# A first layer whose matrix work is woven more finely into its turning steps, with pinned statistics and joined additions

## The chip, the cores and the metric

One Trainium2 chip, one of its cores. The metric is the device time of one execution in microseconds (us). A core has five engines with instruction queues of their own: TensorE (PE in the profile; its weight loads are PEld), VectorE (DVE), ScalarE (ACT), GpSimd (POOL), and SyncE (SP), which here issues DMAs. [...] SBUF is the working memory on the chip, PSUM the memory into which TensorE writes, in 8 banks of 512 floats for each of 128 partitions.

## The reference, cut to what matters

The network has four layers, each `x = x + layer(group_norm(x))`, on x of 8 images of 56 x 56 positions and 192 channels, in float32. The change is in the first layer alone. Cut to it:

```python
x = gn(x)                                   # 32 groups of 6 channels, per image
p = silu(x @ p_w.T + p_b)                   # 576 channels each
q = silu(x @ q_w.T + q_b)
v = silu(x @ v_w.T + v_b)
qv = q * v
o1 = toeplitz(qv along w, a1)               # per channel a causal-anticausal filter of the row
o2 = toeplitz(qv along h, a2)               # and of the column; a1, a2 from a small MLP
x = x_in + (p * (o1 + o2)) @ o_w.T + o_b
```

The filters are per channel 56 x 56 Toeplitz matrices, so `o1 + o2` is, for each channel and image, two small matrix products.

## The kernel before

**Tiles and stages.** The layer goes image by image (`b`, 8 of them), and in an image through the 576 channels of qv in nine slices of 64, taken two at a time: five steps `c` = 0 to 4, of which c = 4 (the *tail*) has one slice. A step of the loop has these parts:

- `turn_both` (L404; for the tail `turn`, L423, transposes L433, copies L440): seven steps of 8 rows of the product qv. Each has 16 TensorE transposes (L414) into one PSUM tile, and two copies out of it, by VectorE into `ol` and by ScalarE into `or` (L419). The two copies of one tile follow each other.
- `project` (L342): the *gates* of the next step's q and v. For each of four groups `g` of 392 x 2 positions, two PSUM tiles (q and v; one, holding both in its halves, for the tail) of six matmuls each (L358, twelve rows in the profile, as each float32 matmul is shown twice), then Silu by ScalarE (L369) into `s` tiles, then the products `multiply` (L378): one in `straight` order by VectorE (L381), two `across` by POOL (L387); of the last group POOL does one half of the latter and VectorE the other (L387 as well).
- `convolve` (L444): the Toeplitz products, 64 small matmuls in a PSUM tile (L457), two tiles for each slice; tile 0 is evicted into `ot` by VectorE (L477), tile 1 by ScalarE (L475); both engines (L468) for the tail. Each reads everything that was turned.
- `post` (L488), made after c = 1 and c = 3, each time for the four slices of two steps: gate p (L499, L506), turn back and multiply (`back`, L518, L523), output projection (`out`, L532; `rest`, L553; `alone`, L564), and additions into the accumulators `acca` and `accb` (`add`, L481). It runs beside the turning of the next step (c = 2 and c = 4). `post_tail` (L596) does the same for the tail, beside the turning of the next image's c = 0: `gates` (L606, matmuls L612, Silu L618), `back` (L627, L632), `out` (L640), `rest` (L655), with twelve additions (L486), each for one parity of image rows.
- `normalize` (L668) of the next image's x runs in c = 2, in three parts: `measure` (12 `bn_stats`, L156), `deviate` (aggregates L160, mean L161, spreading matmuls L129, variance), `last` (matmuls L129, Sqrt L170, reciprocal L171, L172, then the affines L49 and L680). `tell` (L686) measures the finished image for the next layer: 11 `bn_stats` in c = 0, its `deviate` and `last` in c = 1.

**PSUM.** Tiles are pairs of banks: three buffers `c`, taken in turn, and one `o`. `banks()` (L204) gives an `o` for each fourth tile while `ring["wide"]` holds (c = 0, 1, 3), and only `c` in c = 2 and 4, where `out` has the `o`. The gates' results and the gated p lie in six `s` buffers of SBUF.

**What sets the order.** TensorE's order in this layer is the program's (L712): it is written out with `merge` (L699), which spreads two lists of steps over each other. Within a pass of the loop: `merge(fill + early gates, turns)`, where `fill` are the steps of `post` or `post_tail`; then the early groups' products; then the other groups of `project`, merged with `beside` (parts of `tell` and `normalize`); then the convolutions, each second one followed by the DMAs that fetch the next Toeplitz tables (`toeplitz`, L324, L334). Before, two groups of gates were *early*, and only where there was no `fill` (c = 1 and c = 3, and the very first c = 0). At c = 3 the remaining groups alternate with convolutions. The order of VectorE, ScalarE, POOL and SP is chosen when the program is built, by a scheduler that reorders what the dependencies allow; each queue is then fixed and runs in order. Semaphore waits are inserted by the framework.

**Lines that move.** In SP's queue of an image's c = 0 are the store of the finished accumulators (L71), the load of the next image (L89), the load of the new accumulators (L73), and the Toeplitz tables for later convolutions (L334).

The core of the loop, as it was:

```python
early = [] if fill else ahead[0:2]
ring["wide"] = c not in (2, 4)
merge(fill + [f for f, _ in early], turns)
ring.update(at=0, wide=True)
for _, f in early:
    f()
ahead = whole(ahead[len(early) :])
```

Of the kernel before, what the change touches and what calls it, by code (L numbers as in the profile page):

```python
# [99 lines left out]
class GroupNormSplit:  # L100
# [40 lines left out]
    def steps(self, *spans):  # L141
# [12 lines left out]
        def measure(x, n, st, j):  # L154
            w = x.shape[-1] // n
            nc.vector.bn_stats(st[:, j, :], x[:, j * w : (j + 1) * w])  # L156
# [21 lines left out]
def layer0(cx, xin, xout, w, consts):  # L178
# [15 lines left out]
    with ExitStack() as es:  # L194
# [147 lines left out]
        def project(xn, q):  # L342
# [9 lines left out]
            def gates(g):  # L352
                pss = []
                for i in range(len(js)):
                    ps = banks()
                    for k in range(3):
                        for h, rows in enumerate(halves):
                            nc.tensor.matmul(  # L358
                                ps[:, h, 0:n], wqv[q][rows, k, i, :],
                                xn[rows, k, g * n : (g + 1) * n],  # L360
                                start=(k == 0), stop=(k == 2),
                            )
                    pss.append(ps)
                ts = []
                for i in range(2):
                    j, ps = js[0 if tail else i], pss[0 if tail else i]
                    rows = slice(i * DS, (i + 1) * DS) if tail else slice(0, 128)
                    t = work(2, n)[0 : DS if tail else 128]
                    nc.scalar.activation(t, ps[rows, :, 0:n], AF.Silu, bias=bqv[rows, j : j + 1])  # L369
                    ts.append(t)  # L370
                state[g] = ts
# [4 lines left out]
            return [(lambda g=g: gates(g), lambda g=g: products(g)) for g in range(4)]  # L376
# [219 lines left out]
        def post_tail(xn, ot, acc):  # L596
# [6 lines left out]

            sps, pos = [], []

            def gates():  # L606
                for g in range(2):
                    ps = banks()
                    for k in range(3):
                        for p in range(2):  # L610
                            for h in range(2):
                                nc.tensor.matmul(  # L612
                                    ps[sides[p], h, 0:n], wps[2][sides[h], k, 0, 0:DS],
                                    rows(xn[sides[h], k], g * 7, p),
                                    start=(k == 0), stop=(k == 2), skip_group_check=True,
                                )
                    sp = work(2, n)
                    nc.scalar.activation(sp, ps[:, :, 0:n], AF.Silu, bias=bp[:, NC - 1 : NC])  # L618
                    sps.append(sp)
# [15 lines left out]
            def out(g):  # L635
                po = pos[g]
                for h in range(2):
# [6 lines left out]
                    for p in range(2):  # L644
                        add(
                            0, NC - 1, rows(acc[0], h * 14 + g * 7, p),
                            pa[:, p, 0:n].rearrange("p (i w) -> p i w", w=H),
                        )

            def rest(g):  # L650
# [8 lines left out]
                for p in range(2):  # L659
                    add(  # L660
                        1, NC - 1, rows(acc[1], g * 7, p),
                        pb[:, p, 0:n].rearrange("p (i w) -> p i w", w=H),
                    )

            steps = [lambda f=f, g=g: f(g) for f in (back, out) for g in range(2)]
            return [gates, *steps, lambda: (rest(0), rest(1))]

        def normalize(xn):  # L668
# [7 lines left out]
            def last():  # L676
                rstd, nbias = settle(banks)
                for k in (0, 2):
# [7 lines left out]
        def tell(b, xa, xb):  # L686
# [3 lines left out]
            def last(bank):  # L690
                nn = cx.tile(gn.small, [128, 2, 2], "nn")
                for i, v in enumerate(settle(bank)):
                    nc.vector.tensor_copy(nn[:, :, i], v)
# [23 lines left out]
        def whole(steps):  # L717
            return [lambda f=f, h=h: (f(), h()) for f, h in steps]
# [1501 lines left out]
```

## Time and profile before

| | |
|---|---|
| median of 3 runs | 4062.32 us (4058.22 to 4072.35) |
| the profiled execution | 4069.0 us, its span 4067.2 |
| mean granted TensorE clock | 0.981 |
| TensorE busy in the span | 3786.1 us (93%) |
| weight loads | 2655.7 us (65%) |
| VectorE | 2371.5 us (58%) |
| ScalarE | 1789.6 us (44%) |
| POOL | 1523.3 us (37%) |
| images of the first layer, from one c = 0's first turning step to the next | 235.0, 234.9, 235.3 us (images 2 to 4) |
| the same for TensorE busy | 219.7, 218.1, 219.3 us |
| one `bn_stats` of 392 elements (L156) | 0.545 us; four in a row 1.96 |
| one gate's Silu (L369), 784 elements | 0.91 us |
| a turned tile's copies (L419) | VectorE 1.21, ScalarE 1.01 us |
| an activation table load | 1.283 us |
| VectorE's straight product (L381) | 0.97 us, 1.6 beside POOL |
| POOL's across product (L387), 392 elements | 1.93 us mean |
| the tail's additions before (L486, 392 elements) | 0.55 us, in a row 0.49 |

The times are of one profiled execution, from the span's start. In the groups and the timeline a row names line, engine, operation, output and inputs, and the idle time of the engine just before with what ended it. The matmuls' ends are modelled, so a TensorE row may overlap the next by 0.1 to 0.2 us. The first layer fills the span to about 1940 us.

### The profile page before, as it was taken

To read this page: it belongs to the slowest core of one execution; us is meant where nothing else is said; L and a number is where in the kernel's file an instruction comes from. 1 tells how busy PE (TensorE), PEld (TensorE's weight loads), DVE (VectorE), ACT (ScalarE), POOL (GpSimd) and SP (SyncE) were. 2 spreads that over 40 slices of the span, in tenths; PEclk is the share of its full clock that TensorE was granted. 3 is DMA by queue.
4 is the path that set the end of the run, shared out by engine and by line. 5 is a ranking of instruction groups with operands and counts; after the bars stand their busy time and mean duration, and the time that the engine had idled before them with its cause. 6 is when DMAs were issued, how large, how long until landed. Compare 5 with 4: busy or idle time off the path is not lost. (4 is left out here: it accounts for less than half of the span.)

```text
span 4067.2 us, 115859 instructions
## 1 busy us (share of the span) xinstructions
PE 3786.1 (93%) x51036; PEld 2655.7 (65%) x51036; DVE 2371.5 (58%) x3318; ACT 1789.6 (44%) x2021; POOL 1523.3 (37%) x1325
## 2 busy tenths in 40 slices
PE   6989999999998999999799999899989999998997
PEld 4777767677776767777566666444435455556997
DVE  6556565655657565555544444565566667665654
ACT  2434444344444434443334433243335555554564
POOL 3222242222233222223433333333334444444776
PEclk9999999999999999999899999999999999999999
DMA  7865353533526352342333443556557766653333
GB/s 158 169 143 131 81 142 103 125 77 98 125 76 160 85 136 72 89 105 76 108 104 103 107 104 94 167 166 209 166 163 184 181 153 154 153 132 102 99 99 98
DMA packets 390300, 507.94 MB, mean 125 GB/s; under 512 B 176932, under 2 KB 326724, under 8 KB 388404
## 3 DMA queue, kind: packets, MB, share of 16 engines
q1 hardware_dynamic: 385621, 494.07, 47.6%
q8 instruction: 401, 6.57, 0.7%
q10 hardware_dynamic: 3135, 3.47, 0.3%
q0 software_dynamic: 1040, 2.99, 0.3%
q14 instruction: 103, 0.84, 0.1%
HBM read 344.69 MB, written 155.65 MB: 123 GB/s over the span
## 5 line engine op out<-in xcount | busy, mean ns | idle before, releaser
L387 POOL TENSOR_TENSOR qv<-s,s 128x392 f32<-128x392 f32 (+3 forms) x320 | 569.3, 1806 | 1296.4 <-ACT s L369 1048.5
L358 PE MATMUL c<-x,wqv 64*128 64x392 f32 x2856 | 518.3, 509 | 45.9 <-ACT or L419 24.7
L358 PEld LDWEIGHTS c<-x,wqv 64*128 64x128 f32 x2856 | 285.0, 193 | 223.6 <-ACT or L419 29.8
L369 ACT ACTIVATE s<-c,bqv 128x784 f32<-128x784 f32 (+1 forms) x270 | 244.9, 913 | 330.0 <-PE c L358 308.1
L381 DVE TENSOR_TENSOR qv<-s,s 128x784 f32<-128x784 f32 (+1 forms) x160 | 229.0, 1441 | 132.0 <-ACT s L369 132.0
L499 PE MATMUL c<-x,wp 64*128 64x224 f32 x2688 | 282.1, 356 | 17.0 <-ACT s L506 14.4
L419 DVE COPY ol<-c 56x1024 f32<-56x1024 f32 x184 | 218.7, 1208 | 113.6 <-PE c L414 113.6
L499 PEld LDWEIGHTS c<-x,wp 64*128 64x128 f32 x2688 | 254.5, 189 | 21.7 <-ACT s L506 16.6
L523 DVE TENSOR_TENSOR s<-s,c 128x896 f32<-128x896 f32 x112 | 121.8, 1088 | 239.6 <-ACT s L506 233.3
L419 ACT COPY or<-c 56x1024 f32<-56x1024 f32 x184 | 184.0, 1008 | 175.8 <-DVE ol L419 169.5
L457 PEld LDWEIGHTS c<-or,ol 120*64 120x64 f32 x7168 | 217.3, 139 | 40.4 <-issue 38.0
L457 PE MATMUL c<-or,ol 120*64 120x56 f32 x7168 | 225.3, 224 | 19.3 <-issue 10.1
L2084 POOL TENSOR_TENSOR y<-y,s 128x448 f32<-128x448 f32 x168 | 185.2, 1102 | 95.8 <-ACT s L2063 95.8
L1552 ACT ACTIVATE vb<-sm 128x1024 f32<-128x1024 f32 (+1 forms) x100 | 103.9, 1040 | 261.1 <-issue 218.2
L2053 PE MATMUL h<-ringv,am 128*64 128x57 f32 (+1 forms) x4400 | 192.7, 235 | 21.8 <-DVE ringv L2040 13.9
L506 ACT ACTIVATE s<-c,bp 128x448 f32<-128x448 f32 x224 | 129.7, 630 | 185.5 <-PE c L499 184.1
L1541 PE MATMUL v<-wvb,wa 128*128 128x512 f32 (+1 forms) x400 | 192.1, 613 | 6.4 <-ACT wa L1427 6.4
L2053 PE MATMUL h<-ringh,am 128*64 128x57 f32 (+1 forms) x4400 | 186.3, 232 | 8.8 <-DVE ringh L2059 8.8
L2053 PEld LDWEIGHTS h<-ringv,am 128*64 128x64 f32 x4400 | 168.1, 140 | 25.4 <-DVE ringv L2040 14.9
L1060 PE MATMUL c<-wv,xc 128*126 128x192 f32 x896 | 175.4, 339 | 0.0
L2053 PEld LDWEIGHTS h<-ringh,am 128*64 128x64 f32 x4400 | 166.3, 139 | 11.1 <-DVE ringh L2059 11.1
L1570 POOL TENSOR_TENSOR l<-vb,ta 128x512 f32<-128x512 f32 (+1 forms) x52 | 75.2, 1446 | 259.5 <-ACT vb L1552 258.5
(268 smaller groups left out, 7708.7 us busy)
## 6 DMA issues: line engine op xcount, KB each, us to landing
or<-tt SPq DMA_DIRECT2D x252, 196.0 KB
ol<-tt SPq DMA_DIRECT2D x252, 196.0 KB
vt<-v SPq DMA_DIRECT2D x56, 672.0 KB
v<-vb SPq DMA_DIRECT2D x96, 384.0 KB
x<-x SPq DMA_DIRECT2D x110, 168.0 KB
wqv<-in_l_w_qv SPq DMA_DIRECT2D x38, 384.0 KB
x<-in_x SPq DMA_DIRECT2D x64, 196.0 KB
x<-x SPq DMA_DIRECT2D x110, 112.0 KB
```

The source lines that it names most:

```text
L358: nc.tensor.matmul(ps[:, h, 0:n], wqv[q][rows, k, i, :], xn[rows, k, g * n : (g + 1) * n], start=(k == 0), stop=(k == 2),)
L369: nc.scalar.activation(t, ps[rows, :, 0:n], AF.Silu, bias=bqv[rows, j : j + 1])
L381: nc.vector.tensor_tensor(sub(qv[rows, 7 * g :, 64 + H - 1 :], (HH * 120, 2), (120, 7), (-1, H)), *(t.rearrange("p u (h w) -> p u h w", w= ...
L387: eng.tensor_tensor(sub(qv[rows, w0:, H - 1 - 7 * g - HH * u :], (120, w1 - w0), (-1, 7)), *(t[:, u].rearrange("p (h w) -> p w h", w=H)[:, ...
L419: copy(dst[:, :, :, i0 : i0 + 8], view[rows])
L457: nc.tensor.matmul(ps[u * 64 : (u + 1) * 64, k, v * H : (v + 1) * H], left[:, d * H : d * H + 64], right[:, d * H : (d + 1) * H], start=Tr ...
L499: nc.tensor.matmul(ps[:, h, u * n : (u + 1) * n], wps[j][rows, k, u, :], xn[rows, k, g * n : (g + 1) * n], start=(u == 0 and k == 0), stop ...
L506: nc.scalar.activation(sp[:, u].rearrange("p (h i) -> p h i", h=2), ps[:, :, u * n : (u + 1) * n], AF.Silu, bias=bp[:, 2 * j + u : 2 * j + ...
L1060: nc.tensor.matmul(out(i, u), group(i, u), wv[0], start=(u == 0), stop=True, skip_group_check=True,)
L1541: nc.tensor.matmul(out, x[:, at : at + n], wt, start=(k == 0), stop=(k == 1), skip_group_check=True,)
L2053: nc.tensor.matmul(ps[sides[c], y], am[a][:, m * CB : (m + 1) * CB], old[:, x], start=(n < 2), stop=True, skip_group_check=True,)
L2084: nc.gpsimd.tensor_tensor(v, v, line[:, j], ALU.add)
```

## The change

- **Gates tile by tile.** `project` returns for each group a list of gate steps, one for each PSUM tile, where one step did both tiles. In the tail's gates the one tile is followed by its two Silus as before.
- **More early groups, and in another place.** The number of early groups now depends on c alone: two for c = 0 and 1, three for c = 3, none for 2 and 4. So c = 0 of every image has two early groups beside the tail's `post_tail`. The early gates are first merged with `fill`, then the result with the turning steps.
- **The tail's stage.** `post_tail`'s two gate tiles become two steps. `out` and `rest` add both parities of rows in one instruction of 784 elements, so twelve additions become six.
- **Statistics pinned.** Each `bn_stats` of `gn.steps` is pinned behind everything that the program has traced for VectorE before it. So those of the next image stand in c = 2, behind group 0's product, where the scheduler had placed them in c = 0; those of the finished image stand behind the products of groups 2 and 3 in c = 0.
- **ready.** After the reciprocal of the statistics, ScalarE applies Silu to one element of it, pinned in ScalarE's order. This puts the Silu table's load behind the Sqrt at once; before, it came with the next Silu that was needed. It is done in `normalize` and, except for the last image, in `tell`.

The number of TensorE, POOL and SP instructions is the same; VectorE has 48 fewer, ScalarE 15 more. The queues of VectorE, ScalarE and SP come out in another order: among others, in c = 1 both early straight products stand ahead of the copies of the last two turned tiles, and in c = 0 one stands ahead of the copy of turning step 4 and one ahead of that of step 6; in SP's queue of c = 0 the new accumulators' load stands behind the Toeplitz tables, where it stood ahead of them.

```diff
         def measure(x, n, st, j):
             w = x.shape[-1] // n
-            nc.vector.bn_stats(st[:, j, :], x[:, j * w : (j + 1) * w])
+            cx.tc.keep_in_program_order(
+                nc.vector.bn_stats(st[:, j, :], x[:, j * w : (j + 1) * w])
+            )
...
-            def gates(g):
-                pss = []
-                for i in range(len(js)):
-                    ps = banks()
-                    for k in range(3):
...
-                    pss.append(ps)
-                ts = []
-                for i in range(2):
...
-                    ts.append(t)
-                state[g] = ts
+            def gate(g, i):
+                ps = banks()
+                for k in range(3):
...
+                j = js[i]
+                for rows in halves if tail else [slice(0, 128)]:
                     t = work(2, n)[0 : DS if tail else 128]
                     nc.scalar.activation(t, ps[rows, :, 0:n], AF.Silu, bias=bqv[rows, j : j + 1])
+                    state.setdefault(g, []).append(t)
...
-            return [(lambda g=g: gates(g), lambda g=g: products(g)) for g in range(4)]
+            return [
+                ([lambda g=g, i=i: gate(g, i) for i in range(len(js))], lambda g=g: products(g))
+                for g in range(4)
+            ]
...
+            def pairs(x, r0):
+                return x.rearrange("q (i p w) -> q p i w", p=2, w=H)[:, :, r0 : r0 + 7, :]
...
-                    for p in range(2):
-                        add(
-                            0, NC - 1, rows(acc[0], h * 14 + g * 7, p),
-                            pa[:, p, 0:n].rearrange("p (i w) -> p i w", w=H),
-                        )
+                    add(
+                        0, NC - 1, pairs(acc[0], h * 14 + g * 7),
+                        pa[:, :, 0:n].rearrange("q p (i w) -> q p i w", w=H),
+                    )
...
-            steps = [lambda f=f, g=g: f(g) for f in (back, out) for g in range(2)]
-            return [gates, *steps, lambda: (rest(0), rest(1))]
+            steps = [lambda f=f, g=g: f(g) for f in (gate, back, out) for g in range(2)]
+            return [*steps, lambda: (rest(0), rest(1))]
+
+        def ready(v):
+            t = cx.tile(gn.small, [1, 1], "ready")
+            tc.keep_in_program_order(nc.scalar.activation(t, v[0:1, 0:1], AF.Silu))
...
                 rstd, nbias = settle(banks)
+                ready(rstd)
...
-                early = [] if fill else ahead[0:2]
+                early = ahead[0 : {0: 2, 1: 2, 3: 3}.get(c, 0)]
                 ring["wide"] = c not in (2, 4)
-                merge(fill + [f for f, _ in early], turns)
+                woven = []
+                merge(
+                    [lambda f=f: woven.append(f) for f in fill],
+                    [lambda f=f: woven.append(f) for fs, _ in early for f in fs],
+                )
+                merge(woven, turns)
```

## The prediction

> **What bounds the kernel now.** I read the page's busy shares, then one image of the first layer in windows, then the timelines of TensorE, VectorE and ScalarE around each place where TensorE idles, then the granted clock.
>
> ```profile
> PE 3786.1 (93%) x51036; PEld 2655.7 (65%) x51036; DVE 2371.5 (58%) x3318; ACT 1789.6 (44%) x2021; POOL 1523.3 (37%) x1325
> ```
>
> ```profile
> 1000.20:1235.10 234.90, 218.13 (x3160) 171.86 (x3156) 142.88 (x174) 102.07 (x120) 70.94 (x40) 0.99 0.42 107
> ```
>
> The second view is one image of the first layer (c=0's first turning step to the next image's): length, then busy us and instructions of PE, PEld, DVE, ACT, POOL, the granted clock, the DMA share, GB/s. TensorE works 218 of 234.9 us, VectorE 143, ScalarE 102, POOL 71. So TensorE's queue sets the time, and a change counts only where it opens or closes a TensorE gap. The layer runs to about 1940 us; the other three follow it and are only shifted. Per image the gaps sit in five places, the same in every image to 0.1 us: c=0's turning stage and the wait behind it (3.74 + 0.74), c=1 behind the turning (1.86), c=2's start (2.2) and end (0.52 + 0.84), c=3's turning (0.61 + 1.17 + 1.25), c=4 (0.3); and a gap of 2.0 to 3.25 in c=0's convolutions in images 1 to 6.
>
> ```profile
> 919.87 0.69 PE L414 MATMUL c<-ident,qv 64*120 64x64 f32 x16 [1.17 <-ACT s L369]
> ...
> 921.82 3.88 PE L358 MATMUL c<-x,wqv 64*128 64x392 f32 x12 [1.25 <-ACT or L419]
> ...
> 1039.49 1.20 PE L457 MATMUL c<-or,ol 120*64 120x56 f32 x33 [3.25 <-issue]
> ...
> 1056.65 4.22 PE L358 MATMUL c<-x,wqv 64*128 64x392 f32 x24 [1.86 <-ACT or L419]
> ...
> 1076.95 1.28 ACT L506 ACT_TABLE_LOAD   x1 [1.61 <-PE c L499]
> ...
> 1079.45 2.54 PE L499 MATMUL c<-x,wp 64*128 64x224 f32 x24 [1.65 <-ACT s L506]
> ...
> 1145.61 2.25 PE L358 MATMUL c<-x,wqv 64*128 64x392 f32 x12 [0.84 <-DVE ot L477]
> ```
>
> The columns are start, length, engine, line, operation, operands, count, and the idle time before with what ended it. The reader sees, in c=3 (the first two rows), turning steps that wait for ScalarE, and twelve gate matmuls that take 3.88 us where a later dozen takes 2.25; in c=1 a gate waits for a PSUM buffer until VectorE (1.22 us) and then ScalarE (1.01 us) have copied a turned tile; in c=2 the activation table load delays the first gate's Silu, and so the next gate by 1.65.
>
> The place that decides is c=2, where the next image is normalized:
>
> ```profile
> 1025.11 1.96 DVE L156 BATCH_NORM_STATS2 st<-x 128x6 f32<-128x392 f32 x4
> ...
> 1029.30 2.14 PE L358 MATMUL o<-x,wqv 64*128 64x392 f32 x12
> ...
> 1123.05 0.98 DVE L381 TENSOR_TENSOR qv<-s,s 128x784 f32<-128x784 f32 x1 [3.80 <-ACT s L369]
> ...
> 1123.81 2.14 PE L358 MATMUL o<-x,wqv 64*128 64x392 f32 x12
> ...
> 1125.78 1.62 PE L129 MATMUL c<-mean,gmat 64*128 64x1 f32 x28
> ...
> 1127.45 0.16 DVE L137 COPY spread<-c 128x3 f32<-128x3 f32 x1 [3.42 <-PE c L129]
> ```
>
> The mean's matmuls (L129) start without a gap, because their input was ready 93 us earlier: the statistics of x (L156) ran at 1022 to 1033, in c=0, beside full TensorE work.
>
> **What the Trainium skill says.** "TensorE: Matmul & The Clock Gate", "Part 1: The HAM clock gate", has TensorE at half rate after an idle window of about 3.4 us. The trace agrees on the length (records of 3.413 us at half clock, one from 921.7 to 925.1, under the 3.88 us row) and is finer: in this layer half of a window idle is enough. Windows 0.47 to 0.71 idle were followed by a half one; each costs about 3.4/2 = 1.7 us. The same page ("Architectural detail") has VectorE and ScalarE as strict queues and only weight loads pulled ahead on TensorE; the trace shows no exception. "SBUF — State Buffer", "Who interferes with whom": a VectorE instruction with two SBUF inputs contends with a POOL instruction that reads SBUF. The trace agrees: L381 takes 0.97 alone and 1.6 beside POOL's L387. "ScalarE: Activation LUTs", "What ACT_TABLE_LOAD costs": about 1283 ns plus a drain; the trace has 1283 and no drain (1076.95 to 1078.24).
>
> **The change part by part**, in the instruction order of the built program. n counts images.
>
> *Statistics pinned.* The 12 L156 of the next image now stand in c=2, behind the product L381 of gate group 0, followed by 3 aggregates and the mean; TensorE's order there is unchanged (groups 0 and 1, then the mean's matmuls). VectorE can't pass L381, which ends at 1124.0. Four L156 take 1.96, so 12 take 5.85: 1129.85. Aggregates 3 x 0.22, mean 0.16 (POOL is through by 1130.3): 1130.8. TensorE is there at 1125.95, so it stands for 4.85 us, with every later matmul behind it. n = 7 (images 0 to 6): **+34**. If the mean copy takes 0.73, as once in c=0, it is +37; at the least, with aggregates overlapped, +31. The clock: a 4.85 us gap always leaves one window over half idle, in most positions two; averaged over its position a half window behind it costs 1.7: **+12** (7 to 17). Taking 5.85 us of L156 from c=0 gives nothing, since TensorE waits for no VectorE work there.
>
> *The tiny Silu (ready).* It moves the Silu table load up behind the Sqrt. In c=2's start the 1.28 us load goes. Image 0, which has no statistics to finish there, shows what is late next: its stage idles 1.41, not 2.20. So -0.8, n = 7: **-5.5**; two half-clock windows there (behind 840 and 1550 us) go: **-3.4**. In c=2's end the load lies under the wait of 2.45 us for nbias; group 3's products come 1.28 earlier, the eviction L477 ends before TensorE asks, 0.84 goes, n = 7: **-6**. Its cost: ScalarE waits for the reciprocal (1072.1), so L475 starts 1.4 us late; its buffer isn't asked for before 1086. At the program's start, two L156 leave the chain to the first affine: **-1**.
>
> *Gates among turning steps, c=1.* TensorE's order becomes gate, turn, gate, turn, turn, gate, turn, turn, gate, turn, turn. But VectorE's order has both early products L381 ahead of the last two turned tiles' copies, and the second waits for the fourth gate's activation. Walking the queues with 1.97 a gate, 0.51 a turn, 1.2 + 1.0 a tile's two copies, times from the stage's first gate: the fourth gate ends at 10.65, its Silu (behind a turn's copy) at 12.4; L381 beside POOL to 14.05; the copy of turn 5 to 15.2, ScalarE's to 16.2. The next group's first tile waits 0.9 for its buffer, its second 1.8. The same walk with the order of before gives 1.6 where 1.86 is seen. So 2.7 for 1.86, n = 8: **+7** (-8 if the product found no wait).
>
> *c=0, the tail's stage.* Four gates (7.9 us of TensorE) move between the turns. VectorE's work there is about as long as before (six additions of 0.95 for twelve of 0.49; two L156 out, two L381 in), so a stage bound by VectorE becomes one bound by TensorE, up to its end. The walk finds two waits: 1.4 at the second image half of `out`, behind product 0 and turn 4's copies, and 3.0 for group 2's first gate, as product 1 waits for the last gate and turn 6's copies (1.2 + 1.0) queue behind it. Against 4.48 before, less what a later start takes: group 2 starts 1.2 earlier. n = 7: **-8.5** (-25 to 0). A gap of 3.0 makes a half window in some 8 of 10 positions, where two of 7 had one: **+6**. The additions alone save at most six starts, nothing on TensorE's path.
>
> *c=3.* A third early gate needs two ScalarE activations (1.83) among copies of 1.0: ScalarE binds. The walk has the convolutions end at 22.65 behind the stage's start against 22.9: n = 8, **-2**. Half windows there in 5 of 8 images become rarer and partly hidden: **-5**. POOL's products start with the last turning step as before, in every stage, and take 15.7 us (14.5 here); the next turning asks for them 20 us later in c=0 and c=1, but only some 15 later here: the cover is 1 to 2 us.
>
> *SP's queue.* The loads of the next accumulator (12 DMAs, 2.4 MB) fall behind the 16 table loads, and so out of the stretch in which c=0's convolutions wait for "issue". Images 0 and 7, which have one transfer less there, show no such gap. I read it as late instruction supply under full DMA (share 1.05 at 1032 to 1036) and give it a chance of half: half of 6 x 2.7 and two half windows, 20, is **-10** (-20 to +5: c=1's convolutions may be hit by the moved loads).
>
> Sum: 34 + 12 - 5.5 - 3.4 - 6 - 1 + 7 - 8.5 + 6 - 2 - 5 - 10 = +17.6. The profiled execution took 4069.0 (span 4067.2, 1.8 around it), which is 6.7 over the median of the runs, 4062.3, and inside their spread. 4069 becomes 4086.6; from the median, **4080**.
>
> **Rivals.** *Balance* (0.25): the "issue" gaps go entirely (-10 more) and the new half windows fall kindly (-6): +2, 4064. For it: images 0 and 7. Against: the moved loads meet c=1's convolutions.
> *Faster: the turning stages close* (0.15): products wait for nothing, and the gaps of c=0, c=1 and c=3 shrink by 3, 1.9 and 1.5 (-21, -15, -12), ten half windows go (-17), the table loads -12.5, the start -1, against +46: -33, 4030. It decides once the turning stages give more than 3.5 us an image beyond the table loads' share. For it: TensorE then has 13 us of work in c=1 against 8.5 of VectorE. Against it: VectorE's order.
> *Worse* (0.12): "issue" gaps stay (+10), each stall brings two half windows (+7), c=0's end waits for L477 behind six L156 (+5): +40, 4102.
> That the statistics don't move is excluded by the built order.
>
> **The numbers.** Forecast 0.48 with 4066 to 4094 of its own, rivals 0.25, 0.15, 0.12. About 0.3% (12 us) is what a measurement can tell from no change. Slower by more: 0.38 of the forecast and 0.12 and a little of balance, 0.54; within: 0.28; faster: 0.18. The range leaves out the lower half of the faster rival and the tail of the worse one: 4038 to 4104.
>
> **What would show it.** At c=2 of images 0 to 6 a TensorE gap of 4.5 to 5.3 ahead of L129's mean, ended by VectorE's mean, with twelve L156 in a row before it; a half-clock record behind it. No table load at c=2's first gate, its gap near 0.5; no 0.84 before c=3. In c=1 a gap near 1.8 before the second late gate, ended by ScalarE's copy. In c=0 a gap of 2 to 3 before group 2's gates. If the gap at L129 is missing, or c=1's and c=0's gaps are closed, the forecast is wrong, on the fast side.

## The result: slower by 0.9%, and the profile after

| | before | after |
|---|---|---|
| median of 4 runs | 4066.49 us (4058.22 to 4072.35) | 4102.74 us (4100.94 to 4106.13) |
| ratio after to before, 95% interval | | 1.0092 (1.0070 to 1.0113) |
| the profiled execution's span | 4067.2 us | 4103.9 us |
| end of the first layer in it | 1943.2 us | 1980.8 us |
| half-clock records before that end, in sum | 64.8 us | 112.6 us |

The sign was as forecast; the size was twice the forecast, +36 us for +17.6. (A fourth run of the kernel before has moved its median from 4062.3 to 4066.5.) 4102.7 lies above the 4066 to 4094 that the forecast claimed for itself, and 1.3 us inside the end of the whole range, 4038 to 4104. In the trace the layer, counted to the next layer's first `wv` matmul, ends 37.6 us later, and the rest of the span is shifted, not longer.

For the gates and the one-column matmuls a count such as x28 is of rows of the profile, two for each matmul; "28 matmuls" in the text below are such rows.

The page of the changed kernel, part 1, its columns as before:

```profile
PE 3807.7 (93%) x51036; PEld 2663.6 (65%) x51036; DVE 2353.5 (57%) x3270; ACT 1794.8 (44%) x2036; POOL 1502.8 (37%) x1325
```

The same image as before (the fifth) in one window, from c=0's first turning step to the next image's:

```profile
1027.10:1266.17 239.07, 222.90 (x3160) 174.51 (x3156) 140.55 (x169) 102.67 (x122) 67.86 (x40) 0.97 0.42 106
```

TensorE has the same 3160 rows, yet is busy 222.9 us for 218.1: the same matmuls took longer. The granted clock, 0.99 before, is 0.97. The image is 4.2 us longer, of which 4.8 is busy time; the sum of its gaps is about what it was. So the reader should look for two things: where a new gap is, and where the clock fell behind it.

The timeline of TensorE in the changed kernel, at c=0's end, in c=1 and at c=2's start:

```profile
1042.85 1.59 PE L641 MATMUL c<-s,wo 64*128 64x392 f32 x8 [1.01 <-DVE acca L485]
...
1051.55 7.89 PE L358 MATMUL c<-x,wqv 64*128 64x392 f32 x36 [3.19 <-DVE accb L485]
...
1086.04 2.25 PE L358 MATMUL c<-x,wqv 64*128 64x392 f32 x12 [1.84 <-ACT or L418]
...
1105.42 2.54 PE L498 MATMUL c<-x,wp 64*128 64x224 f32 x24 [0.37 <-ACT s L505]
```

The two waits that the prediction's walk found for c=0 (1.4 and 3.0) are there with 1.01 and 3.19, and the 36 rows of three gates take 7.89 us behind the second where 6.2 is usual: a half-clock window. c=1's second late gate waits 1.84. The 1.65 us behind the table load is 0.37.

The place that decides, c=2, in the timeline of VectorE and TensorE of the changed kernel:

```profile
1149.75 0.98 DVE L380 TENSOR_TENSOR qv<-s,s 128x784 f32<-128x784 f32 x1 [3.80 <-ACT s L366]
...
1150.65 5.71 DVE L157 BATCH_NORM_STATS2 st<-x 128x6 f32<-128x392 f32 x12
...
1156.26 0.50 DVE L162 BATCH_NORM_AGGREGATE mv<-st 128x2 f32<-128x24 f32 x3
1156.79 0.17 DVE L163 COPY mean<-mv 128x3 f32<-128x3 f32 x1
...
1157.11 2.83 PE L129 MATMUL c<-mean,gmat 64*128 64x1 f32 x28 [4.46 <-DVE mean L163]
...
1159.73 6.51 PE L358 MATMUL c<-x,wqv 64*128 64x392 f32 x24
```

Twelve statistics in a row stand between product and mean, and TensorE waits 4.46 us, in images 0 to 6 alike. Behind it the mean's 28 matmuls take 2.83 us (1.62 before) and the next 24 gate matmuls 6.51 (4.20 before). The windows there, with the columns of the image's line above:

```profile
1154.10:1157.50 3.40, 0.39 (x8) 0.42 (x8) 2.83 (x9) 0.00 (x0) 2.82 (x2) 1.00 0.00 0
1157.50:1164.30 6.80, 6.80 (x38) 5.21 (x39) 1.60 (x6) 0.20 (x1) 0.00 (x0) 0.50 0.00 0
1164.30:1167.70 3.40, 3.40 (x42) 2.78 (x40) 0.00 (x0) 2.13 (x3) 0.37 (x1) 0.99 0.00 0
```

In the first TensorE works 0.39 of 3.40 us; the next 6.80 us, all of them busy, are granted a clock of 0.50.

### The profile page after: what moved, and what is told of

Read it like the earlier page. It is cut to its first block, busy times and chain, and to the rows that moved or that the text cites. A ratio compares the mean times of both kernels' runs of the same rounds, so it can differ in the third digit from the quotient of the medians.

```text
span 4103.9 us, 115812 instructions
## 1 busy us (share of the span) xinstructions
PE 3807.7 (93%) x51036; PEld 2663.6 (65%) x51036; DVE 2353.5 (57%) x3270; ACT 1794.8 (44%) x2036; POOL 1502.8 (37%) x1325
## 5 line engine op out<-in xcount | busy, mean ns | idle before, releaser
L386 POOL TENSOR_TENSOR qv<-s,s 128x392 f32<-128x392 f32 (+3 forms) x320 | 547.1, 1736 | 1355.1 <-ACT s L366 961.9
L358 PE MATMUL c<-x,wqv 64*128 64x392 f32 x2772 | 527.4, 525 | 57.0 <-DVE accb L485 22.3
L2065 PEld LDWEIGHTS h<-ringh,am 128*64 128x64 f32 x4400 | 166.2, 139 | 10.8 <-DVE ringh L2071 10.5
L531 PE MATMUL o<-s,wo 64*128 64x224 f32 x1536 | 170.6, 359 | 0.0
```

Of the source, the lines that this page charges most:

```text
L358: nc.tensor.matmul(ps[:, h, 0:n], wqv[q][rows, k, i, :], xn[rows, k, g * n : (g + 1) * n], start=(k == 0), stop=(k == 2),)
L386: eng.tensor_tensor(sub(qv[rows, w0:, H - 1 - 7 * g - HH * u :], (120, w1 - w0), (-1, 7)), *(t[:, u].rearrange("p (h w) -> p w h", w=H)[:, ...
L531: nc.tensor.matmul(outs[q][:, h, i * n : (i + 1) * n], wo[rows, 2 * j + u, 0:CA], gated[g][rows, u, h * n : (h + 1) * n], start=(i == 0 an ...
L2065: nc.tensor.matmul(ps[sides[c], y], am[a][:, m * CB : (m + 1) * CB], old[:, x], start=(n < 2), stop=True, skip_group_check=True,)
```

## The experiments

Two theories stood against each other. **A**: the pinned statistics cost the time, as their 5.7 us hold the mean that TensorE waits for, with the half clock behind it; and the woven turning stages give little because VectorE has early products ahead of turned copies. **B**: the weaving of gates among turning steps costs it, and the stall in c=2 only takes up slack that would open elsewhere. Later runs also tell two readings of the clock apart: one-column matmuls count for it as work (**C1**) or as idle time (**C2**). Ratios are to the kernel before on the same chip. Stage lengths are means of images 1 to 6 in the profiled execution, in us, each stage from its own first turning step to the next stage's.

| kernel | median us | ratio (95%) | c=0 | c=1 | c=2 | c=3 | c=4 | image | layer's end | half clock |
|---|---|---|---|---|---|---|---|---|---|---|
| before | 4066.5 | 1 | 46.8 | 30.8 | 71.1 | 25.5 | 61.8 | 235.9 | 1943.2 | 64.8 |
| after | 4102.7 | 1.0092 (1.0070 to 1.0113) | 44.0 | 33.0 | 77.2 | 25.1 | 59.8 | 239.0 | 1980.8 | 112.6 |
| unpinned | 4094.9 | 1.0064 (1.0040 to 1.0087) | 51.0 | 33.4 | 69.2 | 25.6 | 59.8 | 238.9 | 1975.1 | 108.7 |
| pin alone | 4110.3 | 1.0107 (1.0084 to 1.0131) | 42.4 | 31.4 | 80.0 | 25.8 | 61.8 | 241.4 | 1986.1 | 136.5 |
| statistics first | 4103.5 | 1.0097 (1.0076 to 1.0118) | 43.7 | 33.1 | 77.1 | 25.0 | 59.8 | 238.7 | 1976.0 | 112.6 |
| products last | 4071.7 | 1.0005 (0.9995 to 1.0015) | 39.5 | 31.6 | 77.2 | 26.1 | 59.8 | 234.2 | 1947.4 | 98.7 |
| statistics ahead | 4054.3 | 0.9960 (0.9944 to 0.9976) | 43.9 | 33.0 | 70.5 | 25.0 | 59.8 | 232.2 | 1927.7 | 64.8 |
| a third ahead | 4082.2 | 1.0033 (1.0024 to 1.0042) | 44.2 | 33.1 | 74.1 | 25.0 | 59.8 | 236.3 | 1958.6 | 92.2 |
| small matmuls | 4160.2 | 1.0223 (1.0198 to 1.0249) | 47.8 | 31.3 | 82.0 | 26.4 | 61.8 | 249.2 | 2051.4 | 184.3 |
| both | 4026.0 | 0.9887 (0.9869 to 0.9906) | 39.6 | 31.6 | 70.5 | 25.8 | 59.8 | 227.3 | 1896.5 | 57.7 |
| both, no ready | 4028.4 | 0.9905 (0.9889 to 0.9920) | 39.4 | 31.6 | 72.4 | 26.6 | 59.8 | 229.8 | 1907.7 | 58.0 |
| both, two early | 4004.9 | 0.9852 (0.9827 to 0.9876) | 39.5 | 31.6 | 70.3 | 24.0 | 59.8 | 225.1 | 1877.9 | 34.1 |
| both, mean later | 4005.7 | 0.9852 (0.9833 to 0.9872) | 39.4 | 31.6 | 69.2 | 26.6 | 59.8 | 226.6 | 1886.6 | 41.0 |
| all | 4005.1 | 0.9847 (0.9830 to 0.9863) | 39.4 | 31.6 | 69.2 | 25.0 | 59.8 | 225.0 | 1874.5 | 37.5 |

"Half clock" is the sum of the half-clock records before the layer's end. With gates split by tile, the first turning steps of c=0 and of c=1 come one gate (2.0 us) earlier, and the borders with them: 2 us pass from c=4 into c=0 and from c=0 into c=1 without any work changed. So c=4, c=0 and c=1 are best read as a sum; the borders of c=2 and c=3 have not moved.

### Unpinned

```diff
-            cx.tc.keep_in_program_order(
-                nc.vector.bn_stats(st[:, j, :], x[:, j * w : (j + 1) * w])
-            )
+            nc.vector.bn_stats(st[:, j, :], x[:, j * w : (j + 1) * w])
```

> The changed kernel with the statistics unpinned again, the rest as it is (undoes that one part). Theory A (the pinned statistics hold the mean that TensorE waits for): the gap of 4.46 us ahead of the mean's matmuls and the half-clock windows behind it go, 7 x (4.46 + 3.4) = -55. But in the built order the statistics now stand among c=0's turned copies, product 0 and the tail's additions (four ahead of product 0, one or two between the additions, seven ahead of the next product): 2 to 5 us more of VectorE ahead of what TensorE asks for at c=0's end, 7 x 3.5 = +25. So 4103 - 55 + 25 = 4073 (4050 to 4090). Theory B (the weaving of gates among turning steps, with its half windows at c=0's end, costs the time; the stall at c=2 only takes up slack that would open elsewhere): 4103 within 8, with new gaps of about 8 us an image in c=2 or c=3.

Measured: 4094.9, 8 us under the changed kernel, with overlapping intervals: above A's range and just outside B's, so the time alone decides nothing. Both halves of A's expectation are in the table, and the second was too small: c=2 gives 8.0 us an image (77.2 to 69.2; 7.9 expected), but c=0 takes 7.0 back (44.0 to 51.0; 3.5 expected). The new gaps that B put in c=2 or c=3 are not there: TensorE's gaps fall from 6.4 to 2.0 us an image in c=2 and are 3.5 and 3.7 in c=3. The timeline of VectorE of this kernel in c=0, and then what its answer on the statistics' line (L156) says they waited for, with us and times:

```profile
1026.37 1.97 DVE L156 BATCH_NORM_STATS2 st<-x 128x6 f32<-128x392 f32 x4 [0.96 <-DMA x<-in_x]
1028.26 0.96 DVE L378 TENSOR_TENSOR qv<-s,s 128x784 f32<-128x784 f32 x1
1029.13 1.21 DVE L416 COPY ol<-c 56x1024 f32<-56x1024 f32 x1
1030.27 0.95 DVE L483 TENSOR_TENSOR acca<-c,acca 128x784 f32<-128x784 f32 x1
1031.15 0.55 DVE L156 BATCH_NORM_STATS2 st<-x 128x6 f32<-128x392 f32 x1
```

```profile
  DMA x<-in_x: 25.2, 14
```

Without the pin the scheduler puts the next image's statistics among the copies and additions that TensorE waits for in the woven stage, and VectorE, whose queue runs in its built order, stands there for the load of x. Of the fourteen waits two, 9.8 us, are at the program's start, as are all three of the kernel before (8.7 us); the other twelve, 15.4 us, are in c=0, two an image. TensorE's two waits for the additions there grow from 4.2 to 7.5 us an image, and the half clock from 3.4 to 10.8. So the pin has a reason once the stage is woven, and undoing it only exchanges one bad place for another.

### The pin alone

In the kernel before, nothing else:

```diff
-            nc.vector.bn_stats(st[:, j, :], x[:, j * w : (j + 1) * w])
+            cx.tc.keep_in_program_order(
+                nc.vector.bn_stats(st[:, j, :], x[:, j * w : (j + 1) * w])
+            )
```

> The kernel before with the statistics pinned in VectorE's order, nothing else (does that one part alone). TensorE's order is that of before. Theory A: before + 7 x (4.46 + 3.4) = +55, 4121 (4108 to 4130), with a TensorE gap of about 4.5 ahead of the mean's matmuls in seven images and the table load's gaps of 1.65 and 0.84 still there. If the half windows behind the stall are the one that I forecast and not the two or three that the changed kernel shows, +46: 4112. Theory B: 4066 within 12.

Measured: ratio 1.0107, +44 us. B had 4066 and falls. TensorE in c=2 of this kernel:

```profile
1160.61 3.15 PE L129 MATMUL c<-mean,gmat 64*128 64x1 f32 x28 [4.46 <-DVE mean L163]
```

The gap is the same 4.46 in seven images; c=2 grows by 8.9 us an image, but c=0 shrinks by 4.4, which A had left out: the gaps by "issue" (TensorE idle, with nothing in the profile that it waits for), nearly all in c=0, fall from 16.0 to 4.8 us (images 1 to 7), about 2.1 us an image of images 1 to 6, the turning waits by 1.1 us an image, and the half windows there vanish. A's 55 was too large by what c=0 gains.

### Statistics first, and a place that moved with them

```diff
+                if c == 2 and more:
+                    beside.pop(0)()
                 merge(ahead, beside)
```

> The changed kernel with the twelve statistics of the next image put ahead of c=2's first gates, pinned as before, where VectorE is idle for 3.8 us as TensorE works on gate group 0. The mean's matmuls then stand behind group 0 alone. Theory A: the stall shrinks from 4.46 to 0.6 to 1.8, and its half windows go in nearly all images: 7 x (-3.3 - 3.1) = -45, 4058 (4048 to 4070). Theory B: 4103 within 8, since VectorE's work in the stage is the same.

Measured: 4103.5, no gain at all, the gap at 4.43. On its face this is B's number. The timeline of this kernel says why it is not:

```profile
1140.18 4.12 PE L358 MATMUL c<-x,wqv 64*128 64x392 f32 x24
1148.73 2.86 PE L129 MATMUL c<-mean,gmat 64*128 64x1 f32 x28 [4.43 <-DVE mean L163]
...
1151.39 4.33 PE L358 MATMUL o<-x,wqv 64*128 64x392 f32 x12
```

```profile
1141.47 5.70 DVE L157 BATCH_NORM_STATS2 st<-x 128x6 f32<-128x392 f32 x12
1147.09 0.49 DVE L162 BATCH_NORM_AGGREGATE mv<-st 128x2 f32<-128x24 f32 x3
1147.61 0.97 DVE L163 COPY mean<-mv 128x3 f32<-128x3 f32 x1
```

The statistics start 4.8 us earlier in the stage (1.3 behind its first gate, 6.1 in the changed kernel). But with one step fewer to spread, `merge` put the mean's matmuls behind 24 rows of gates instead of 48: TensorE asks for the mean 4.0 us earlier too (4.1 behind the stage's first gate for 8.1), and the mean's copy, beside POOL, takes 0.97 for 0.17. The two cancel. What counts is the distance between the two places.

### Statistics ahead, the mean's matmuls in their place

```diff
+                if c == 2 and more:
+                    beside[0]()
+                    beside[0] = lambda: None
                 merge(ahead, beside)
```

> The changed kernel with the twelve pinned statistics ahead of c=2's gates, as before, but with the mean's matmuls kept where they were, behind gate group 1 (the run that put the statistics ahead had also moved the mean's matmuls a group forward, and TensorE then stood for 4.43 us as before). TensorE asks for the mean 8.1 us behind the stage's first gate. The statistics can start 1.3 behind it and take 5.7, aggregates 0.5, the mean's copy 0.2 to 1.0: ready at 7.7 to 8.5. Theory A (it is the place of the statistics against that of the mean's matmuls that costs): the gap falls from 4.46 to at most 0.5 and the half windows behind it go: 7 x (4.2 + 3.5) = -54, 4049 (4040 to 4062), below the kernel before. Theory B (some other thing in c=2 takes the stall's place, as VectorE does the same work there): above 4075.

Measured: ratio 0.9960, 4054.3, as A expects and below the kernel before. TensorE and VectorE in c=2 of this kernel:

```profile
1112.95 5.70 DVE L157 BATCH_NORM_STATS2 st<-x 128x6 f32<-128x392 f32 x12
...
1119.09 1.02 DVE L163 COPY mean<-mv 128x3 f32<-128x3 f32 x1
```

```profile
1111.66 6.09 PE L358 MATMUL c<-x,wqv 64*128 64x392 f32 x36
...
1120.26 1.73 PE L129 MATMUL c<-mean,gmat 64*128 64x1 f32 x28 [0.53 <-DVE mean L163]
1121.82 4.23 PE L358 MATMUL c<-x,wqv 64*128 64x392 f32 x24
```

The gap is 0.53 and the gates behind it run at 4.23. c=2 is 6.7 us shorter, the other stages are what they were: nothing takes the stall's place. The weaving is not changed in this run, so B's "slack that would open elsewhere" is refuted.

### The clock behind the stall: a smaller dose, and small matmuls alone

Four of the twelve statistics ahead, eight in their place (`measure` takes a number):

```diff
+                if c == 2 and more:
+                    beside[0](4)
                 merge(ahead, beside)
```

> The changed kernel with four of the twelve statistics ahead of c=2's gates and eight where they were; the mean's matmuls in their place. A smaller dose of the same stall: product 0 ends 6.1 us behind the stage's first gate, eight statistics take 3.8, aggregates and the copy 0.5: the mean at 10.4, a gap of 2.3 where 4.46 was. What the clock then does tells two readings apart. C1: only the gap counts as idle; 2.3 us gives a half window in about two of three images, 2.3 us of half clock an image (8.0 in the changed kernel, which C1 puts at 4.5). C2: the mean's one-column matmuls behind the gap count as idle too, so 2.3 + 1.6 to 2.8 give 4 to 5 us of half clock an image. Time: 4103 - 7 x (2.1 + 2.8) = 4069 by C1, 4103 - 7 x (2.1 + 1.7) = 4076 by C2; the records tell more than the time.

The kernel before, with the normalization's spreading matmuls repeated:

```diff
-            for k in ks:
+            for k in ks * (3 if n == 3 else 1):
```

> The kernel before with each of the mean's and the deviation's one-column matmuls in the first layer's normalization done three times over (84 for 28, same result), and no wait added. 56 more matmuls at 1.62/28 us take 3.3 us, 16 times: +52, 4118. C1 (TensorE at work on one-column matmuls counts as busy for the clock): no half-clock record behind them, 4118. C2 (they count as idle): each lot of 4.9 us gives one or two half windows, about 4.9 us of half clock worth 2.5 us, 14 to 16 times, and the matmuls themselves slower: 4150 to 4165.

Measured: with a third ahead, a gap of 2.90 (2.3 expected), and a half-clock record behind it in every image, 3.41 us in six and 6.83 in one: 3.9 an image. As an estimate from the windows counted below, a stretch that counts as idle makes, over all positions, about as much half clock as it is long. So for a gap of 2.9 C1 gives 2.9 and C2 4.6 to 5.7, and 3.9 lies between; the time, 4082, lies above what either gave (4069 and 4076). The second run settles it: 4160, in C2's range, 42 us above C1's. The timeline of TensorE and windows of that kernel (image 4):

```profile
1200.70 5.77 PE L129 MATMUL c<-mean,gmat 64*128 64x1 f32 x84
1206.33 6.52 PE L358 MATMUL c<-x,wqv 64*128 64x392 f32 x24
```

```profile
1200.80:1204.20 3.40, 3.40 (x67) 3.40 (x64) 0.00 (x0) 0.91 (x1) 3.32 (x3) 1.00 0.02 5
1204.20:1211.00 6.80, 6.80 (x38) 4.70 (x38) 1.60 (x6) 0.35 (x1) 0.94 (x1) 0.50 0.00 0
```

In 1200.8 to 1204.2 TensorE is busy for all of 3.40 us, with one-column matmuls and nothing else, and no gap is near; the next 6.8 us are granted 0.50. A half-clock record stands behind the mean in seven of seven images, in none of the kernel before (28 matmuls, 1.62 us). So work of this shape counts for the clock as idle time, and a stall ahead of it is lengthened by it: 4.46 + 1.62 is nearly two windows of 3.41, and at half clock the 28 matmuls take up to 3.15.

All windows of the first layer in the fourteen traces, the two kernels' and the twelve runs', say the same. The half-clock records begin and end on one grid of 3.41 us in each trace. With one-column matmuls taken as idle, no window at full clock that was under 0.43 idle was followed by a half one, and every one over 0.59 was; between, both occur (7310 windows, 231 followed by a half one). Taken as busy, windows without any idle time would have set the clock down in the run with small matmuls. And a window that is itself at half clock needs less: from 0.17 idle on, another half one followed, below that a full one (351 windows, one against it). That is how a stall of 4.46 us, with the matmuls behind it, gets a second half window in every image and a third in three of seven. What exactly the clock weighs stays open; that it is the columns streamed is the obvious guess and was not tried.

### Products last

```diff
-                nc.vector.tensor_tensor(
+                tc.keep_in_program_order(nc.vector.tensor_tensor(
...
-                )
+                ))
```

> The changed kernel with the straight products held in program order on VectorE, so that in c=0, c=1 and c=3 they stand behind the last turned tiles' copies, not between them. Theory A says that this order of VectorE is why the weaving gains so little: c=1's gaps 2.56 to about 0.7 (8 x -1.85 = -15), c=0's 4.20 to about 1.2 (7 x -3.0 = -21), the half window behind c=0's end gone in most images (-10): -46, 4057 (4048 to 4080; above 4070 if the product, now later, holds up the group that comes next). Theory B: weaving the gates itself makes c=0's end late, whatever the place of the products; the idle time there stays at 4 to 5 us an image and the time within 8 of 4103. The stall of 4.46 in c=2 stays in both.

Measured: 4071.7, the kernel before's time. c=0 falls by 4.4 us an image with its half window (31 over seven), c=1 by 1.5 (of 1.85: 0.5 goes to a wait for `tell`'s deviation that is late next). c=3 gives 1.0 an image back, which I had not expected: its convolutions' eviction now stands behind later products, and the wait for it grows from 1.5 to 2.1 us. TensorE and VectorE at c=0's end of this kernel:

```profile
1024.98 1.59 PE L641 MATMUL c<-s,wo 64*128 64x392 f32 x8 [0.51 <-ACT or L418]
...
1031.36 6.20 PE L358 MATMUL c<-x,wqv 64*128 64x392 f32 x36 [0.87 <-ACT or L418]
```

```profile
1029.05 1.22 DVE L418 COPY ol<-c 56x1024 f32<-56x1024 f32 x1 [0.51 <-PE c L413]
1030.19 1.84 DVE L485 TENSOR_TENSOR accb<-c,accb 128x784 f32<-128x784 f32 x2
1031.95 1.22 DVE L380 TENSOR_TENSOR qv<-s,s 128x784 f32<-128x784 f32 x1
```

The products stand behind the last copy and the additions; of 3.19 us 0.87 is left, and the 36 rows of gates take 6.20, not 7.89. TensorE's order is unchanged in this run. So not the weaving, but VectorE's order under it, makes c=0's end late.

### Both, and what is left: the tiny Silu, the third early group, the mean's place

"Both" joins the two edits shown as "products last" and "statistics ahead".

> The changed kernel with both mends: statistics ahead of c=2's gates with the mean's matmuls in their place, and the straight products behind the turned copies on VectorE. Theory A: the two add up, as they lie in different stages: 4103 - 54 - 32 = 4017 (4008 to 4030), faster than both kernels, by 1.2% against the kernel before. If part of one is taken back by the other (a group's product that is now late, a half window that falls elsewhere): up to 4045.

Measured: 0.9887. The two add up, as far as can be measured: the layer's end came 33.4 us earlier with the one and 53.1 with the other, which makes 1894.3; it is 1896.5. By the ratios it makes 0.9874; it is 0.9887.

From "both", without the tiny Silu:

```diff
                 rstd, nbias = settle(banks)
-                ready(rstd)
...
-                if b + 1 < B:
-                    ready(told[0])
```

> The doubly mended kernel (4026) without the tiny Silu, in both places where it stands. My prediction's terms for it: c=2's start idles 2.2 instead of 1.45 (7 x 0.75), the gap of about 0.84 ahead of c=3 opens again (7 x 0.84) and one to three half windows with them: +13 to +18, 4039 to 4044. Rival: the gaps open but other waits behind them shrink by as much, as TensorE only comes later to what VectorE holds up anyway: 4026 within 5.

The gaps come back as put: c=2's start 0.87 to 1.94 us (a turning wait ahead of it shrinks by 0.32), 0.95 ahead of c=3 in place of none; the layer ends 11.2 us later (13 to 18 expected). By the ratios, 0.9905 to 0.9887, the intervals overlap, and the median, 4028.4, is one that the rival allowed (4026 within 5). So one trace of each kernel shows the gain; the times do not prove it.

From "both", with two early groups at c=3:

```diff
-                early = ahead[0 : {0: 2, 1: 2, 3: 3}.get(c, 0)]
+                early = ahead[0 : {0: 2, 1: 2, 3: 2}.get(c, 0)]
```

> The doubly mended kernel with two early groups at c=3 instead of three, as the kernel before has. The third early group adds a gate's two activations to ScalarE, which binds in that stage, and the wait for the convolution's eviction (L476) behind it of 1.5 to 2.5 us is new. If the third group costs, as the stage's length of 25.8 against 25.5 in the kernel before hints: 8 x (-0.3 to -1.5), 4014 to 4024. If my prediction's sign holds (the third group gains 0.25 a stage and half windows, 7 in all): 4033.

Measured: 0.9852, below the 4014 to 4024 expected, with c=3 1.8 us shorter and its half windows gone (2.3 to 0 us an image): the third group costs. c=3's end in "both", then in this kernel:

```profile
690.24 2.54 PE L498 MATMUL c<-x,wp 64*128 64x224 f32 x24 [2.53 <-DVE ot L476]
```

```profile
682.91 2.54 PE L498 MATMUL c<-x,wp 64*128 64x224 f32 x24
```

With three groups early a single group of gates is left beside the convolutions, and `post` asks for a PSUM buffer before VectorE, behind the products, has evicted it. With two, there is no gap.

From "both", with two empty steps in place of one, so that the mean's matmuls stand behind group 2:

```diff
                     beside[0]()
-                    beside[0] = lambda: None
+                    beside[0:1] = [lambda: None] * 2
```

> The doubly mended kernel with the mean's matmuls one gate group later in c=2 (behind group 2), the deviation's behind group 3. The 0.53 us ahead of the mean goes, and the half window that this gap and the 1.7 us of one-column matmuls together still set off in four of seven images: 7 x -0.53 and 4 x -1.7, -10.5: 4015. But the two normalizing instructions then stand between the two convolution evictions on VectorE, and wait there for ScalarE and the reciprocal: if c=3's first turning or gate waits for the second eviction, up to 2 us an image come back: 4030.

Measured: 0.9852, better than the 4015 expected; by the layer's end -9.9 for -10.5 expected. c=2 loses the gap and its half windows, c=3 gains 0.7 us.

"All" has this edit and the one with two early groups on top of "both":

> All mends at once: statistics ahead of c=2's gates, the mean's matmuls a group later, products behind the turned copies, two early groups at c=3. c=2 falls from 70.3 to 69.2 as in the run with the mean later, c=3 stays at 24.0 as in the run with two early groups: 7 x -1.1 = -8 against the latter, about 3997 or a ratio of 0.983. If with two early groups the gate ahead of c=3 waits for the convolution's second eviction, which now stands behind the normalizing instructions on VectorE, 1 to 2.5 us an image come back: 4005 to 4014.

Measured: 0.9847, no further gain that can be told from the two runs above. c=2 is 69.2 as expected, but half-clock windows fall into c=3 again (2.3 us an image, none with two early alone), and c=3 takes 1.0 us back with the same gaps. Each of the last three is about 1.5% under the kernel before, and 2.4% under the changed one.

## Why the prediction was right in sign and short in size

The working had four lots of terms. What the two traces give for them, over the layer's eight images:

| lot | predicted | measured |
|---|---|---|
| c=2: the stall | +34 | 7 x 4.46 = +31.2 |
| c=2: the clock behind it | +12 | 103.9 - 79.1 = +24.8 |
| c=2: start, end and half windows there | -14.9 | the rest of +43.8: -12.2 |
| c=0, c=1 and c=4 together, "issue" included | +7 - 8.5 + 6 - 10 = -5.5 | -6.9 |
| c=3 | -7 | -0.5 |
| the program's start | -1 | +1.2 |
| sum | +17.6 | +37.6 |

**Where the sum failed.** First the step "a 4.85 us gap always leaves one window over half idle, in most positions two; averaged over its position a half window behind it costs 1.7: +12". From the mean's first matmul to the first convolution TensorE has no gap in either kernel and the same matmuls; it takes 79.1 us in seven images before, 103.9 after. That is 3.5 us an image, twice the 1.7. The records behind the stall are two windows long in four images and three in three. The mechanism was right and the size was not: I counted the gap alone as idle and the mean's one-column matmuls as work. Worked through over all positions of the grid, with half a window idle as the limit, a gap of 4.46 us costs an estimated 1.7 us when these matmuls count as work and 3.3 when they count as idle, 3.9 with the lower limit inside a half window. (Two windows over half idle then come out in some 4 of 10 positions for 4.85 us, not in most; the 1.7 itself does come out.) The Trainium skill, "TensorE: Matmul & The Clock Gate", "Part 1: The HAM clock gate", says of the warm-up that the hardware doesn't count instructions but watches an activity window. The trace agrees: in the run with small matmuls 3.40 us without a gap, full of one-column matmuls, are followed by 6.80 us at a clock of 0.50.

Second, c=3: "the convolutions end at 22.65 behind the stage's start against 22.9". They ended earlier than that in images 1 to 7, at 20.4 to 21.3, but the walk stopped there. Behind them `post` waits for the eviction of a convolution's tile, 0.9 to 1.8 us, 1.5 in the mean of images 1 to 6, and starts at 22.2 in each:

```profile
1200.64 2.03 PE L456 MATMUL c<-or,ol 120*64 120x56 f32 x64
1203.55 2.54 PE L498 MATMUL c<-x,wp 64*128 64x224 f32 x24 [0.87 <-DVE ot L476]
```

That takes most of the gain back: in the mean of images 1 to 6 the convolutions end 2.0 us earlier than before and the stage is 0.4 shorter; in images 0 and 7 it is 0.8 and 1.3 longer. With products last and two early groups instead of three, the stage is 1.8 us shorter.

**What held.** The stall's place, its cause, its count and, within 0.4, its size. (The case of a mean's copy of 0.73 us should have read +38, and the copy took about 0.7 in four of the eight images before, not once.) c=1: 0.9 and 1.8 were put, 0.72 and 1.84 are there. c=0: 1.4 and 3.0 put, 1.01 and 3.19 measured, with a half window behind it in seven of seven images (8 in 10 put). The tiny Silu: 0.75 and 0.84 us an image, as put.

**What came out right by a wrong or half-known reason.** That the time fell inside the whole range is luck: its upper end stood there for "worse", and most of what that rival put did not happen. The lot of c=0, c=1 and c=4 is near its forecast because two misses cancel: the "issue" gaps there give 13.7 us (10 put, half windows included), which leaves about +6.8 for the woven stages (+4.5 put). "Taking 5.85 us of L156 from c=0 gives nothing" was wrong: the pin alone gave c=0 4.4 us an image in the kernel before, of which the turning waits are 1.1 and the "issue" gaps 2.1, and its removal cost the woven c=0 7.0. I had asked only what TensorE waits for in the kernel before. The "issue" gaps, given a half chance, went from images 1 to 7 (16.0 to 0.1 us; in image 0 one of 1.99 is new in c=1). Not all of them had stood in c=0's convolutions, as I read it: in images 2 and 3 the larger part, 2.02 and 1.25, stood ahead of gates. In the built order of SP's queue, 12 loads of the new accumulators stand ahead of the 16 table loads in the kernel before, 8 in the unpinned one, 5 with the pin alone, none in the changed one; the gaps are 16.0, 5.5, 4.8 and 0.1. That goes with the moved loads as the cause, but none of these runs moves the loads alone.

**The rivals.** The median fell on "worse", at 4102. Of its three parts only one happened, the half windows; the "issue" gaps did not stay and c=0's end waits for no eviction. "Faster" had asked whether the products find no wait: the run with products last is nearly that case in c=0 and c=1, and it brings 31 us. So the deciding mechanism was the one named, VectorE's order. No run has the joined additions alone; what they give by themselves is not shown.

The first and the last image add 12.9 and 4.7 of the 37.6 us. The last has neither a stall nor, before, an "issue" gap, and so shows the woven turning stages by themselves: 3.9 us slower in c=0, c=1 and c=4 together, 1.3 in c=3.

## What to carry to other kernels

When work is pinned or moved on one engine, measure its distance to the instruction that asks for its result on another, and check that the move does not carry that instruction with it. A gap on TensorE cost its own length and then the clock behind it here, and one-column matmuls next to it counted with it. When matrix work is woven more finely, look at the order of the engine that evicts its tiles: products nobody needs yet belong behind the copies for which TensorE waits.

## What the runs showed that I had not expected

- One-column matmuls set the clock down by themselves: with 84 in 4.8 to 6.9 us, without a gap, 3.4 to 10.2 us of half clock began 2.2 to 5.2 us behind the first of them in seven of seven images; with 28 in 1.62 us, none.
- Getting back to full clock took more work than keeping it: windows under 0.43 idle always kept it, half-clock windows of 0.17 idle and more lost another window.
- A gap of 0.53 us ahead of 1.73 us of one-column matmuls was enough for a half window in two images of seven ("statistics ahead") and four of seven ("both"), so it depends on where the windows fall.
- The mean's copy of 128 x 3 elements on VectorE took 0.17 us at the least, and beside one of POOL's across products as long as that product still ran, to within 0.05: 0.59 in "a third ahead", about 0.7 in four images of the kernel before, 0.97 in "statistics first", 1.02 in "statistics ahead" and "both".
